# A graph network's second layer: the nodes' own edges as a dense stage, attributes closed up on the chip

## The chip, the cores and the metric

One core of a Trainium2 chip runs the whole program. Its engines are named PE (matrix products; PEld is its weight load), DVE (vector), ACT (activation), POOL (GpSimd) and SP (sync, which here issues most DMAs). The metric is the device time of one execution in microseconds (us); the time before is the median of three runs.

## The reference

A graph has 12,500 nodes of 64 values and 212,500 edges, sorted by target. 200,000 edges are random pairs in both directions; the other 12,500 are the nodes' own edges (source = target), one for each node. Each edge has 8 attributes and one of 16 types. What is computed, cut to what matters:

```python
h = relu(layernorm(x))
x = x + segment_sum(h[src] @ weight[etype], dst)            # first layer
h = relu(layernorm(x))
msg_in = concat([h[src], h[dst], edge_attr])                # second layer
x = x + segment_sum(relu(msg_in @ W1 + b1) @ W2 + b2, dst)
```

The second layer is done as a = h @ W1[:64] and b = h @ W1[64:128] + b1 for each node, then relu(a[src] + b[dst] + attr @ W1[128:]) for each edge. The sum over a node's edges is taken before the product with W2.

## The kernel before, in words

Edges are handled in tiles of 128, one edge to a partition, and tiles in groups of G = 4. For every tile POOL issues one indirect DMA (`gather`, line 737) that reads the 128 source rows of 64 values into a buffer; 14 such group buffers rotate (`land`, line 303).

**First layer** (`first_layer`, line 960). Own edges need no gather here: they are put into the table directly from the node's row (`begin`, `some`). The other edges are first closed up, that is, moved to the front where own edges were taken out. `compact` (line 487) does it on DVE: the number of places that a word must move is written in binary, and for each bit a mask is taken (`bitwise_and`) and the words are shifted under it (`copy_predicated`). POOL then stores the result to HBM as `edges_c` (source, type and target of each kept edge). `codes` reads it back, turns it on PE and gives `src_c`, the sources by tile. There are 1563 tiles of kept edges; 28 of the 1563 are covered by the first 32 raw tiles, which leaves 1535 gathers. PE multiplies each tile with a one-hot matrix made by ACT, and DVE adds the product into a window of `table`. Every 8 groups two blocks of 128 nodes are done, and `finish` (line 776) multiplies them with the weights of the types, adds x (held in `x_sb`), normalizes, and writes rows a and b to HBM (`a_rows`, `a_early`, `b_rows`).

**Second layer** (`second_layer`, line 1090). It uses all 212,500 edges in their original order: 1661 tiles, 416 groups, with sources `src_i`, targets within the window `local` and `dst_l`, and attributes `attr_t`, all prepared on the host and loaded. For a group, POOL gathers rows of a; PE forms b[dst] + attr @ W1c in one product from a window of 40 b rows plus 8 rows of weights (`b_win`) and a one-hot matrix with 8 rows of attributes under it (`of_edges`); DVE adds the two (`z`), ACT takes the relu (`hid`), PE sums over targets (`pa`), and DVE adds into a window of `sums`. Every 8.5 groups `results` (line 1069) multiplies two blocks with W2, adds x from `x_sb` and writes the output.

**The order.** Each engine's instructions stand in the order in which this code issues them: the class `InOrder` (line 316) hangs each one behind the last of its engine. All these instructions so have line 325 in the profile, and are told apart by their tiles. Preparation runs beside the first layer: generators such as `prepare` and `open_step` are advanced by one step for each tile (`for i in range(G)` at line 1041), and `yield from rest(n)` is a distance of n steps. Since POOL's stores stand in this order too, a store that waits holds back the gathers behind it.

`in_any_order` (line 1218) is a slow path for other kinds of input. It is in the program, but does not run here.

Of the kernel before, what the change touches and what calls it, by code (L numbers as in the profile page):

```python
# [40 lines left out]
F32 = mybir.dt.float32  # L41
# [37 lines left out]
AHEAD2 = AHEAD + 28  # L79
NGR = NT // G  # L80
NTR = -(-E // P)
# [20 lines left out]
LPARTS = EP // (P * LROW)  # L102
LOOPS_UPTO = [0, 2560, 5632, 8704, NB * P]
# [24 lines left out]
BS = 2  # L128
GS2 = 17
# [6 lines left out]
FIN = [-(-GS2 * (k + 1) // 2) + SLACK - 1 for k in range(NREG)] + [408, 412, NGR - 1]  # L136
STEP = [sum(f < g for f in FIN) for g in range(NGR)]
# [5 lines left out]
def bounds():  # L143

    least, most = [(0, 0)], [(0, 0)]
    for k in range(NFIN - 1):
        b0, nb = BLOCKS[k]
        end = (b0 + nb) * P

        x = (FIN1[k] + 1 - SHIFT) * G * P  # L150
        least.append((x + end, end))
        ahead = end + AHEAD - WT
        if x + ahead < E:
            most.append((x + ahead, ahead))
        x = (FIN[k] + 1) * G * P
        least.append((x, end))
        most.append((min(x, E) - 1, end + AHEAD2 - W))

    most.append((RAWE, RAWE - CUT * P))
    most.append((RAWE - 1, SN + AHEAD - WT))  # L160
    for c in range(1, PARTS):
        most.append((c * P * ROW, c * P * ROW - UPTO[c] * P))
    for q in range(1, LPARTS):
        least.append((q * P * LROW, LOOPS_UPTO[q]))
    return least, most
# [28 lines left out]
def gnn_kernel(  # L194
    ctx: ExitStack, tc, x, src, dst, etype, attr, src_t, dst_t, attr_t, rows_c, rows_l, raw_c, raw_f, first, last, step_t, step_c, least, most, w_rel, w1, b1, w2, b2, out
# [11 lines left out]
    dst_l = dram.tile([NGR, G * P], BF16, name="dst_l")  # L207
# [10 lines left out]
    x_sb = keep.tile([P, NB * D], F32, name="x_sb")  # L218
    x3 = x_sb.rearrange("p (b d) -> p b d", d=D)
    tail = N - (NB - 1) * P  # L220

    def load_x(b0, Q):

        full = min(b0 + LB, NB - 1)
        Q.dma_start(x3[:, b0:full, :], x[b0 * P : full * P].rearrange("(b p) d -> p b d", p=P))
        if b0 + LB == NB:
            V.memset(x3[:, NB - 1, :], 0.0)
            Q.dma_start(x3[:tail, NB - 1, :], x[(NB - 1) * P :])
# [3 lines left out]
    NCK = 3 * PARTS + 4 * LPARTS + 4  # L232
# [22 lines left out]
    def layer_norm(pool, b0, nb, name):  # L255
# [44 lines left out]
    def in_order():  # L300
        with ExitStack() as c2:
# [82 lines left out]
            local = own.tile([P, NT], F32, name="local")  # L384
            sums = [own.tile([DA, SN + AHEAD2], F32, name=f"sums{k}") for k in range(2)]
            first_row = own.tile([1, NGR], I32, name="first_row")
            src_i = own.tile([P, NT], I32, name="src_i")

            place_row = own.tile([1, NGR], I32, name="place_row")
            w1ab = own.tile([P, 2, D], F32, name="w1ab")  # L390
            b1_bc = own.tile([P, D], F32, name="b1_bc")
            w2b = own.tile([DA, D], F32, name="w2b")

# [14 lines left out]
            def weights():  # L408
# [5 lines left out]
                Q_.dma_start(t_loop[N:, :].rearrange("n o -> o n"), none)  # L414
                yield
                Q_.dma_start(first_row, first.unsqueeze(0))
                Q_.dma_start(place_row, step_t[::G].unsqueeze(0))
# [18 lines left out]
            def local_targets():  # L436

                n = NGR // RB
                d = prep.tile([n, RB, G * P], I32, name="local_d", bufs=1)
                f = prep.tile([n, RB], I32, name="local_f", bufs=1)  # L440
                o = prep.tile([n, RB, G * P], BF16, name="local_o", bufs=1)
                Q_.dma_start(d, dst[:EP].rearrange("(n g e) -> n g e", n=n, g=RB))
                Q_.dma_start(f, first.rearrange("(n g) -> n g", n=n))
                yield from rest(8)
                for g in range(RB):
                    V_.tensor_tensor(o[:, g, :], d[:, g, :], f[:, g : g + 1].to_broadcast([n, G * P]), op=ALU.subtract)
                    yield
                Q_.dma_start(dst_l.rearrange("(n g) e -> n g e", n=n), o)
                Q_.dma_start(src_i, src_t)
                for t in sums:  # L450
                    V_.memset(t, 0.0)
                V_.tensor_scalar(first_row, first_row, 0.0, float(N), op0=ALU.max, op1=ALU.min)
                V_.tensor_tensor(place_row, first_row, place_row, op=ALU.subtract)
                yield
                V_.tensor_scalar(place_row, place_row, 0.0, float(SN + AHEAD2 - W), op0=ALU.max, op1=ALU.min)
                yield

            def sources_of_last(of, pool):

                for g in of:  # L460
                    s_bc = pool.tile([P, G * P], I32, name="s_bc", bufs=1)
                    Q_.dma_start(s_bc, src[g * G * P : (g + 1) * G * P].unsqueeze(0).to_broadcast([P, G * P]))
# [7 lines left out]
            def locals_of(c):  # L470

                n = NT // NCH
                cs = slice(c * n, (c + 1) * n)
                d = prep.tile([P, n], I32, name="local_e", bufs=1)
                f = prep.tile([P, n // G], I32, name="local_w", bufs=1)
                Q_.dma_start(d, dst_t[:, cs])
                Q_.dma_start(f, first[c * n // G : (c + 1) * n // G].unsqueeze(0).to_broadcast([P, n // G]))
                yield from rest(8)
                V_.tensor_tensor(
                    local[:, cs].rearrange("p (g k) -> p g k", k=G),  # L480
                    d.rearrange("p (g k) -> p g k", k=G),
                    bc(f, 2, G, [P, n // G, G]),
                    op=ALU.subtract,
                )
                yield

# [289 lines left out]
            def finish(k, psA):  # L776
# [3 lines left out]
                long = nb == BS  # L780
                if long:
                    yield from rest(2)
# [21 lines left out]
                x_b = x3[:, b0 : b0 + nb, :]  # L804
                V_.tensor_tensor(x_b, x_b, pT[:, :nb, :], op=ALU.add)
                st = wk.tile([P, nb, 6], F32, name="s_st")
# [3 lines left out]
                for i in range(nb):  # L810
                    V_.bn_stats(st[:, i, :], x3[:, b0 + i, :])
# [81 lines left out]
            def verdict(psA):  # L893
                span = prep.tile([NGR // G, 2, G], I32, name="v_span", bufs=1)
                bad = prep.tile([NGR // G, G], F32, name="v_bad", bufs=1)
# [4 lines left out]
                Q_.dma_start(span[:, 0, :], first.rearrange("(n g) -> n g", g=G))  # L900
                Q_.dma_start(span[:, 1, :], last.rearrange("(n g) -> n g", g=G))
# [4 lines left out]
                V_.scalar_tensor_tensor(  # L906
                    bad, span[:, 1, :], -float(W), span[:, 0, :], op0=ALU.add, op1=ALU.is_ge,
                    accum_out=next(odds_of)[: NGR // G],
                )
# [34 lines left out]
            def beside_part(c, psA):  # L944
# [6 lines left out]
                if c == 1:  # L951
                    yield from local_targets()
                    yield from weights_of_attributes()
                if c == 5:
                    yield from sources_of_last(range(2), wk)
                yield from locals_of(c)
# [3 lines left out]
            def first_layer(psA, loops_0):  # L960
# [5 lines left out]
                open_step, coming, fresh = iter(()), iter(()), iter(())  # L966
                n_of, oh_of, rows_of, pa_of = {}, {}, {}, {}
# [37 lines left out]
                for it in range(NG1 - RAWG + L1_ADD[1]):  # L1005
                    g = it + RAWG
                    if g < NG1:
                        k = (g - SHIFT) * G
                        if it == 0 or k in UPTO:
                            c = sum(k >= b for b in UPTO[1:])  # L1010
                            for _ in coming:
                                next(fresh, None)
                            coming = beside_part(c, psA)
                        if it % 56 == 4 and it // 56 < NB // LB:
                            load_x(it // 56 * LB, Q_)
# [24 lines left out]
                    for j in range(max(len(now), len(adds))):  # L1040
                        for i in range(G):
# [9 lines left out]
                            next(coming, None)  # L1051
                        if j < len(adds) and adds[j] in FIN1:
# [3 lines left out]
                            for _ in fresh:  # L1056
                                next(coming, None)
                            if k + 1 < NFIN:
# [4 lines left out]
                for _ in coming:  # L1063
                    pass
# [3 lines left out]

            def results(k, ps):
                (b0, nb), t = BLOCKS[k], sums[k % 2]  # L1070
                po = ps.tile([P, BS, D], F32, name="po", bufs=1)
# [5 lines left out]
                V_.tensor_tensor(o[:, :nb, :], po[:, :nb, :], x3[:, b0 : b0 + nb, :], op=ALU.add)  # L1077
                if k + 2 < NFIN:
                    V_.memset(t[:, AHEAD2:], 0.0)
# [4 lines left out]
                else:  # L1084
                    S_.dma_start(
                        out[b0 * P : (b0 + nb) * P].rearrange("(b p) d -> p b d", p=P), o[:, :nb, :]
                    )
                yield

            def second_layer(ps):  # L1090
# [3 lines left out]
                open_step = iter(())  # L1094
                a_of, n_of, oh_of, pz_of, hid_of, pa_of = {}, {}, {}, {}, {}, {}
                at, at_b = {}, {}
                of_z, of_hid, of_pe, of_add = (turns(lag, NGR) for lag in (L2_Z, L2_HID, L2_PE, L2_ADD))
                for it in range(NGR + L2_ADD[1]):

                    g = it  # L1100
                    if g < NGR:
                        if g % RG == 0:
                            at_b.update(enumerate(windows(first_row, g, PAD_DST, Q_), g))
                        if g % RB == 0:
                            local_bc = wk2.tile([W, RB * G * P], BF16, name="local_bc", bufs=3)
                            Q_.dma_start(
                                local_bc,
                                dst_l[g : g + RB, :].rearrange("g e -> (g e)").unsqueeze(0).to_broadcast([W, RB * G * P]),
                            )
                            of_edges = wk2.tile([WE, RB * G * P], F32, name="of_edges", bufs=3)  # L1110
                            Q_.dma_start(of_edges[W:, :], attr_t[:, g * G * P : (g + RB) * G * P])
# [571 lines left out]
```

## Time and profile before

| | |
|---|---|
| median of three runs | 4086.79 us (4086.44 to 4087.43) |
| the profiled execution | 4087.75 us, its span 4085.9 us |
| POOL busy | 3083.5 us (75%), 3274 instructions |
| PE busy | 2422.0 us (59%) |
| ACT busy | 1640.5 us (40%) |
| DVE busy | 1146.0 us (28%) |
| granted TensorE clock | 0.523 |
| gathers of the first layer | from 50.9 to 2002.0 us |
| gathers of the second layer | from 2002.4 us; of a_rows from 2022.3 to 4075.7 us |

The page gives for each group of instructions the tiles written and read (out<-in), the shape, how many there are, their busy time, the mean duration of one, and the time that the engine sat idle before them with what ended it. "issue" means that nothing visible was waited for. An indirect DMA on POOL is the time in which POOL builds the transfer; the transfer itself follows. In the line of slices each digit is the busy share, in tenths, of a fortieth of the span.

### The profile page before, as it was taken

Reading aid. Unit: us, or ns where it says so; the run is one execution under the profiler, and the core shown is the slowest. Engines: PE = TensorE matmul, PEld = TensorE weight load, DVE = VectorE, ACT = ScalarE, POOL = GpSimd, SP = SyncE. Lnnn points to the kernel's source line nnn. Section 1 sums busy time; section 2 is a strip of 40 time slices with the busy share of each in tenths; the row PEclk is TensorE's granted clock in tenths of the full one; section 3 lists DMA queues with packets and bytes.
Section 4 is the critical chain, followed back from the end, with each engine's and each line's share of the span. In section 5 each row is a group of like instructions: output and inputs, shape, how many; then the busy total and the mean of one; then the engine's idle time right before and its main releaser. Section 6 shows DMA issues by size and latency. Waiting matters only on the chain. (4 is left out here: it accounts for less than half of the span.)

```text
span 4085.9 us, 49975 instructions
## 1 busy us (share of the span) xinstructions
PE 2422.0 (59%) x14840; PEld 1853.3 (45%) x14840; DVE 1146.0 (28%) x4671; ACT 1640.5 (40%) x3222; POOL 3083.5 (75%) x3274
## 2 busy tenths in 40 slices
PE   1655655555555555556686666666666666666655
PEld 0433333333333333333475555555555555555555
DVE  7533334333333333333211111111111111111111
ACT  6754545454545454545333222322232222322222
POOL 7777777777777777777777777777777777777776
PEclk9655555555555555555555555555555555555555
DMA  4222222121222222121222121111111112111111
GB/s 124 48 44 64 42 48 44 40 46 40 51 40 45 42 45 42 38 41 37 48 46 42 42 42 44 42 42 42 42 42 42 42 41 44 41 42 42 42 39 36
DMA packets 233554, 184.50 MB, mean 45 GB/s; under 512 B 162969, under 2 KB 171680, under 8 KB 232336
## 3 DMA queue, kind: packets, MB, share of 16 engines
q0 software_dynamic: 104320, 107.70, 14.1%
q1 hardware_dynamic: 115655, 70.30, 6.5%
q10 hardware_dynamic: 13298, 3.20, 0.4%
q8 instruction: 121, 1.98, 0.2%
q14 instruction: 160, 1.31, 0.1%
HBM read 162.74 MB, written 18.20 MB: 44 GB/s over the span
## 5 line engine op out<-in xcount | busy, mean ns | idle before, releaser
L325 POOL DMA_INDIRECT rows<-a_rows,src_i x1645 | 1552.2, 944 | 501.4 <-issue 428.9
L325 POOL DMA_INDIRECT rows<-h_rows,src_c x1535 | 1456.9, 949 | 468.2 <-issue 390.4
L325 PE MATMUL pa<-oh_r,rows 128*64 128x96 f32 x6140 | 836.2, 381 | 780.8 <-DMA rows<-h_rows,src_c 701.9
L325 PE MATMUL pz<-b_win,of_edges 48*128 48x64 f32 x3322 | 819.0, 424 | 686.3 <-ACT of_edges L325 682.1
L325 PEld LDWEIGHTS pz<-b_win,of_edges 48*128 48x128 f32 x3322 | 739.3, 324 | 735.7 <-ACT of_edges L325 712.0
L325 PEld LDWEIGHTS pa<-oh_r,rows 128*64 128x64 f32 x6140 | 472.4, 204 | 1193.8 <-DMA rows<-h_rows,src_c 848.8
L325 ACT ACTIVATE hid<-z 128x256 f32<-128x256 f32 x416 | 172.9, 416 | 1429.7 <-DVE z L325 1399.3
L325 DVE TENSOR_TENSOR z<-pz,rows 128x256 f32<-128x256 f32 x416 | 176.3, 424 | 1652.4 <-DMA rows<-a_rows,src_i 1520.3
L325 ACT ACTIVATE off_r<-iota_s,code 128x192 bf16<-128x192 f32 x1535 | 568.1, 441 | 0.0
L325 DVE TENSOR_TENSOR table<-table,pa 128x96 f32 x1567 | 395.6, 252 | 368.6 <-PE pa L325 262.1
L325 PE MATMUL pa<-oh,hid 128*65 128x40 f32 x3322 | 456.8, 312 | 38.3 <-ACT hid L325 27.2
L325 PEld LDWEIGHTS pa<-oh,hid 128*65 128x65 f32 x3322 | 395.9, 226 | 88.6 <-ACT hid L325 30.8
L325 ACT ACTIVATE oh_r<-off_r 128x768 f32<-128x768 bf16 x392 | 330.2, 842 | 211.5 <-PE pa L325 203.6
L325 DVE SCALAR_TENSOR_TENSOR table<-b_rel,rsel,hT 128x256 f32<-128x256 f32 (+1 forms) x400 | 171.6, 467 | 401.8 <-PE hT L325 391.6
L325 ACT ACTIVATE off<-local_bc,neg_w 40x1024 bf16<-40x1024 bf16 x208 | 235.8, 1134 | 21.5 <-DMA local_bc<-dst_l 12.9
L325 ACT ACTIVATE of_edges<-off 40x1024 f32<-40x1024 bf16 x208 | 219.7, 1056 | 6.5
L325 PE MATMUL pT<-table,wrel 128*64 128x256 f32 (+1 forms) x800 | 200.0, 596 | 2.1 <-DVE table L325 2.1
L325 DVE TENSOR_TENSOR oh<-local,iota_p 128x160 f32<-128x160 f32 x416 | 128.5, 310 | 0.0
L325 DVE TENSOR_TENSOR x_sb<-x_sb,pT 128x128 f32<-128x128 f32 (+1 forms) x50 | 14.2, 284 | 394.5 <-PE pT L325 394.5
L325 ACT COPY table<-table 128x1024 f32<-128x1024 f32 x49 | 51.2, 1045 | 143.0 <-DVE table L325 143.0
L325 ACT ACTIVATE s_rs<-s_mv,eps 128x2 f32<-128x2 f32 (+1 forms) x50 | 14.8, 296 | 230.9 <-DVE s_mv L325 230.9
L325 DVE TENSOR_TENSOR sums<-sums,pa 65x40 f32 x416 | 75.2, 181 | 46.1 <-PE pa L325 33.8
(193 smaller groups left out, 1049.6 us busy)
## 6 DMA issues: line engine op xcount, KB each, us to landing
rows<-a_rows,src_i POOLq DMA_INDIRECT x1645
rows<-h_rows,src_c POOLq DMA_INDIRECT x1535
local_bc<-dst_l SPq DMA_DIRECT2D x104, 160.0 KB
of_edges<-in_attr_t SPq DMA_DIRECT2D x104, 64.0 KB
b_win<-b_rows SPq DMA_DIRECT2D x416, 10.0 KB
b_rel<-t_loop SPq DMA_DIRECT2D x48, 128.0 KB
l_in<-in_rows_l SPq DMA_DIRECT2D x4, 1009.5 KB
b_h<-h_rows SPq DMA_DIRECT2D x48, 64.0 KB
```

The costliest lines, as they stand in the source:

```text
L325: last_ins[self.engine] = getattr(self.engine, name)(*args, **kw)
```

## The change

The second layer now uses the closed-up edges of the first: `src_c`, 391 groups (1563 tiles, the last group of three), 8 groups to two blocks. Everything that came from the host for it (`src_t`, `dst_t`, `attr_t`, `first`, `last`) is gone. In its place:

- `places_of` makes `first_row`, `local` and `dst_l` of each part from `edges_c`. It replaces `local_targets` and `locals_of`.
- `kept` closes up the attributes of the kept edges on DVE, four times, 128 rows of 432 edges with 8 words each, and POOL stores them (`attr_c`).
- `loop_attrs` picks out the attributes of the own edges, four times, and POOL stores them (`attr_l`).
- `turn` reads 16 tiles of attributes back (pieces of 8 words), turns them on PE, copies them on ACT and writes `turned_c` or `turned_l`: 99 and 7 times.
- These run beside the first layer: `attrs` takes a step for every second tile, `turns_of_attrs` for every tile.
- `own_edges`, once for two blocks, computes the own edges' relu(a + b + attr @ W1c) densely, turns it and writes it into `sums` before the windows of those blocks are added. The window ahead grows from 156 to 256 columns.
- x is no longer held: `finish` loads two blocks (`x_b`) and writes the sum to HBM (`x_mid`); `results` reads it back (`x_r`).

The core of the diff:

```diff
-AHEAD2 = AHEAD + 28
+BS = 2
+AHEAD2 = BS * P
+KWIN = 432
+KCL = 400
+SUB = 16
+IN_SUB = 3
+            def kept(q):
...
+                a = prep.tile([P, KWIN * EA], F32, name="k_a", bufs=1)
+                load_halves(a, attr, q, EA, KWIN)
...
+                a3 = a.rearrange("p (e c) -> p e c", c=EA).bitcast(I32)
+                for k in range(5):
+                    n = 1 << k
+                    V_.tensor_single_scalar(move, v, n, op=ALU.bitwise_and)
+                    half = KWIN // 2
+                    for e0, e1 in ((0, half), (half, KWIN - n)):
+                        V_.copy_predicated(
+                            a3[:, e0:e1], wide(move[:, e0 + n : e1 + n], [P, e1 - e0, EA]), a3[:, e0 + n : e1 + n]
+                        )
+                        yield
+                    if k < 4:
+                        V_.copy_predicated(v[:, : KWIN - n], move[:, n:], v[:, n:])
+                    yield
+                yield from store(attr_c, to, a[:, : KCL * EA], rest)
+                closed.append(q)
+            def loop_attrs(q):
...
+                for h in range(2):
...
+                    load_halves(a[:, : m * SUB * EA], attr, q, EA, m * SUB, h * m * SUB)
+                    yield from rest(14)
+                    a4 = a[:, : m * SUB * EA].rearrange("p (b e c) -> p b e c", e=SUB, c=EA).bitcast(I32)
...
+                    for k in range(4):
+                        n = 1 << k
+                        V_.tensor_single_scalar(m3, v3, n, op=ALU.bitwise_and)
+                        V_.copy_predicated(
+                            a4[:, :, : SUB - n], wide(m3[:, :, n:], [P, m, SUB - n, EA]), a4[:, :, n:]
+                        )
+                        yield
...
+                for k in range(7):
+                    n = 1 << k
+                    V_.tensor_single_scalar(v2[:, 1], v2[:, 0], n, op=ALU.bitwise_and)
+                    V_.copy_predicated(top_i[:, : last - n], wide(v2[:, 1, n:], [P, last - n, EA]), top_i[:, n:])
+                    if k < 6:
+                        V_.copy_predicated(v2[:, 0, : last - n], v2[:, 1, n:], v2[:, 0, n:])
+                    yield
+                yield from store(attr_l, to, top[:, :LN].rearrange("p s c -> p (s c)"), rest)
+            def turn(of, t0, n, into, psA):
+                t = prep.tile([P, 16, EA], F32, name="u_in", bufs=3)[:, :n]
+                words = of[t0 * P * EA : (t0 + n) * P * EA, :]
+                Q_.dma_start(t, words.rearrange("(t p c) o -> p t (c o)", p=P, c=EA))
+                yield
+                yield from take(bank)
+                by_c = psA.tile([P, P], F32, name="hT", bufs=1)[: n * EA]
+                T_.transpose(by_c, t.rearrange("p t c -> p (t c)"), ident)
+                yield
+                o = prep.tile([P, P], F32, name="u_out", bufs=2)[: n * EA]
+                S_.copy(o, by_c)
+                bank.clear()
+                Q_.dma_start(into[t0 * EA : (t0 + n) * EA, :], o)
+                yield
+            def own_edges(b, t, col, ps):
...
+                for i in range(BS):
+                    T_.matmul(po[:, i, :], lhsT=at[:, i, :], rhs=w1c, start=True, stop=True)
+                yield
+                V_.tensor_tensor(ab[:, 0], ab[:, 0], po, op=ALU.add)
+                V_.tensor_tensor(ab[:, 0], ab[:, 0], ab[:, 1], op=ALU.add)
+                S_.activation(h[:, :, :D], ab[:, 0], AF.Relu)
+                yield
+                pl = both[:DA, : BS * P]
+                for i in range(BS):
+                    T_.matmul(pl[:, i * P : (i + 1) * P], lhsT=h[:, i, :], rhs=ident, start=True, stop=True)
+                yield
+                V_.tensor_copy(t[:, col : col + BS * P], pl)
...
-                        a_of[g], n_of[g] = gather((a_early if g < EARLY else a_rows)[:, :], src_i, g, NTR)
+                        a_of[g], n_of[g] = gather((a_early if g < EARLY else a_rows)[:, :], src_c, g, NTC)
```

In `first_layer`, the two new streams are advanced here (the lines around it are as before):

```diff
                             next(coming, None)
+                            if i % 2:
+                                next(aside, None)
+                            next(turning, None)
```

## The prediction

> **What bounds the kernel now.** I read the busy table first, then the slices, then the groups of POOL by shape, its waits, and last the timeline of POOL and DVE together.
>
> ```profile
> POOL 7777777777777777777777777777777777777776
> L325 POOL DMA_INDIRECT rows<-a_rows,src_i x1645 | 1552.2, 944 | 501.4 <-issue 428.9
> L325 POOL DMA_INDIRECT rows<-h_rows,src_c x1535 | 1456.9, 949 | 468.2 <-issue 390.4
> L325 POOL DMA_INDIRECT edges_c<-c_out,c_to x16 | 14.6, 913 | 4.9 <-issue 4.0 <-DVE table L325 0.6 <-DVE r_mv L250 0.3
> ```
>
> POOL shows the same 7 in every slice. Its 3252 indirect DMAs stand in an unbroken row: (1552.2 + 501.4) / 1645 = 1.248 us from one start to the next in the second layer, 0.944 of it busy and 0.30 issue, and in its list of waits the longest single wait is 0.7 us. PE waits for the gathers in both layers (701.9 us for h_rows; DVE's z 1520.3 us for a_rows). So the time is the number of POOL's indirect DMAs times their pace, and an edit counts if it changes that number or that pace. The chain that ended last begins only behind the last gather, and says no more.
>
> The pace differs a little: 944 ns in the second layer, 949 in the first. The timeline shows why.
>
> ```profile
> 622.06 0.85 DVE L325 SCALAR_TENSOR_TENSOR l_f<-l_f 128x672 f32<-128x672 f32 x1
> 622.26 1.46 POOL L325 DMA_INDIRECT rows<-h_rows,src_c  x1 [0.30 <-issue]
> ...
> 102.19 0.41 DVE L325 COPY_PREDICATED c_v<-c_move,c_v 128x223 int32<-128x223 int32 x1
> 102.25 1.15 POOL L325 DMA_INDIRECT rows<-h_rows,src_c  x1 [0.30 <-issue]
> ...
> 52.85 0.86 DVE L325 MAX8 l_top<-l_f 128x8 f32<-128x672 f32 x1
> 53.40 0.94 POOL L325 DMA_INDIRECT rows<-h_rows,src_c  x1 [0.30 <-issue]
> ```
>
> The columns are start, duration, instruction. A gather that starts while a DVE instruction with two SBUF inputs is under way ends 0.81 to 0.82 us after that instruction's end: 622.06 + 0.85 = 622.91, and 622.26 + 1.46 = 623.72; 102.60 and 103.40. Behind MAX8, one SBUF input and as long, nothing happens (0.94). So a gather is lengthened by (what is left of the DVE instruction at its start) - 0.13 us, and the next gather follows 0.30 us later, so that nothing is caught up. With a gather every c = 1.249 us, at a random place against it, a DVE instruction of length L costs POOL on average (L-0.13)^2/2c if L-0.13 is under c, and L-0.13-c/2 if it is over. Test on this trace: summed over all such instructions of the first layer after 90 us this gives 7.5 us; the gathers there exceed 944 ns by 7.2 us in all. For the formula that is a good match, though with lengths up to 0.86 us only.
>
> **What the change removes from POOL.** The second layer gathers 1547 tiles in place of 1645 (391 groups, the last of three tiles): 98 x 1.248 = **-122.3 us**.
>
> **What it adds to POOL.** Sixteen stores (eight attr_l, eight attr_c), at the edges_c row (14.6 + 4.9) / 16 = 1.22 us: **+19.5**. The t_loop stores, 128 bytes a row, take 914 ns, edges_c, 1.6 KB a row, 913: size does not show. attr_c writes 12.8 KB a row; if that doubled its eight, +7 more.
>
> **What it adds in POOL's way.** Closing up attributes is DVE work with two SBUF inputs, in the first layer. Lengths from these rows:
>
> ```profile
> L325 DVE COPY_PREDICATED c_v<-c_move,c_v 128x223 int32<-128x223 int32 x7 | 2.9, 410 | 0.2
> L325 DVE COPY_PREDICATED c_v<-c_move,c_v 128x208 int32<-128x208 int32 x7 | 2.8, 394 | 0.2
> L325 DVE TENSOR_TENSOR c_f<-c_f 128x224 f32<-128x224 f32 x14 | 5.5, 389 | 0.2
> L325 DVE TENSOR_TENSOR l_f<-l_f 128x672 f32<-128x672 f32 x4 | 3.4, 854 | 0.0
> ```
>
> From 224 to 672 elements 465 ns, so 1.04 ns an element; a predicated copy is 0.178 us + 1.04 n. The program holds, over four parts each of `kept` and `loop_attrs`:
> - 40 predicated copies of 1600 to 1728 elements (a half row of 8 words an edge): 1.85 to 1.98 us, 78 us busy; cost 1.17 to 1.22 each: 47.9.
> - 8 each of 2520, 2352, 2016 and 1344 elements: 2.80, 2.63, 2.28, 1.58 us; cost 2.05, 1.87, 1.52, 0.82: 50.2.
> - 28 of 496 to 1000 elements, 1.08 us on average: 0.37 each: 10.4.
> - 16 tensor_tensor of 672, 0.855 us: 0.21 each: 3.4.
> - the short ones (40 copies of the counts, 8 of 432, 8 of 126, `places_of`): 4.2.
>
> Together 235 us of DVE and **+116 us** of POOL; the removed `local_o` and `local` rows take off 0.7 by the same formula. DVE has room: 723 of 1910 us busy between 90 and 2000 us. The two ends, if the formula's mean fails: the 72 copies over 1.5 us cost at least L-0.13-1.249 each and at most L-0.13, so 0.62 us less or more each, 45 us in all. The 80 one-input mask instructions (bitwise_and, 0.2 to 0.4 us by c_move's 302 ns) hold some gathers too: by the formula +1.3.
>
> The Trainium skill ("SBUF — State Buffer", Who interferes with whom) says that VectorE and GpSimd share a pair of SBUF ports, exclusively and for a whole instruction; but it infers that tensor_tensor does not hold up descriptor generation, only copies and tensor_scalar in a two-port mode do. This trace contradicts that: 1.43 to 1.55 us beside two-input instructions. By the page's inference the added holds would be the 1.3 alone and the time about 3986.
>
> **What lies beside.** Everything else is on engines that wait for POOL, and I cost it at nothing:
> - PE: 106 + 16 transposes in the first layer at 0.40 to 0.48 us (hT, pab rows), some 55 us against 780.8 us of waiting for h_rows; in the second layer 49 times four small products, near 90 us, against 686.3 us of waiting, and 392 products fewer each of pz and pa.
> - ACT: 122 copies of about 0.3 us in the first layer; in the second 49 activations more, 12 pairs off and of_edges fewer.
> - SP and DMA: about 210 issues of 0.4 us for the turning, 50 + 50 + 50 for x_b, x_mid, x_r, 147 for the own rows. A turning read has 2048 pieces of 32 bytes; x_sb's load, 1792 pieces of 256 bytes, is through 5 us after issue, and one such read falls on about 6.5 us. A core's DMA engines are at 0.22.
> - The cover for all this is 14 groups of row buffers, 70 us of POOL: z lags the gathers by 1.7 us in the second layer, and by at most 28 us at its start, where SP now has about eight DMAs more. Without the cover a late load would cost POOL its full lateness.
> - The end: the last group has 3 tiles in place of 1; its pa and z rows (0.31 each product) add under 1 us.
>
> New waits on POOL's queue: the first store of each pair follows its last DVE step at once, and for attr_c also the turning reads in flight; behind it queue the gathers. The table adds that stand at the same place in the order end 8 to 23 us before POOL gets there, and the last step takes 2 us. So 0 now; at worst the 8 to 10 us of that lead each, eight times.
>
> **Sum**, on the profiled execution (span 4085.9, 4087.75 in all): 4087.75 - 122.3 + 19.5 + 116 - 0.7 + 1.3 = 4101.6; where a burst of copies fills DVE, its next copy starts 0.6 to 1.0 us behind the last, before POOL's next start at 1.11, which costs some 0.3 more for about 15 of them: +4.5, so 4106. The runs' median is 1.0 lower: **4105**. POOL's gain is given back beside DVE.
>
> **Rivals.**
> 1. Forecast, the holds cost what the formula says: 4085 to 4130. Chance 0.57.
> 2. Faster: the long copies hold POOL less than the short ones suggest. One mechanism, where a copy starts against a gather: DVE's steps follow PE, which follows the gathers, so a fixed distance could put the start just behind a gather's start. The lower end, -45: 4060. With no hold at all it is 3986. It decides as soon as the holds sum to less than 95 us. For it: no row is over 0.86 us. Against: the 1560 table adds, which pace these steps, end at any place against the gathers (137 to 181 in each tenth), and the 35 c_v copies lie nearly as evenly. Chance 0.21.
> 3. Waits in place of the gain: `kept` brings 25 us of DVE within about eight groups (40 us, 15 busy already), the lead is used up and POOL waits at the first stores, on DVE and on the reads; SP in turn waits for the stores' landing, and the loads behind it come late. Eight times 5 us: 4145; at 10 us, 4185. For it: SP already waits 78.8 us for t_loop stores, longest 28.9. Against: POOL, slowed by the holds, gives DVE more time. Chance 0.22.
> 4. That it does not do what it says: the program's POOL row shows 1547 gathers; no chance given.
>
> **Numbers.** About 0.2% (8 us) is what a measurement can tell from no change. Of case 1 a quarter lies within 8 us of before (4079 to 4095), of case 2 a tenth: same 0.16. Faster 0.19, slower 0.65. The range takes case 2's phase end and case 3's middle: 4060 to 4150; outside lie no hold at all (0.06) and heavy waits (0.08). Both signs hold much, so case 1 alone: 4085 to 4130.
>
> **What would show it.** In the profile after: 1547 a_rows gathers at 944 ns, and h_rows gathers at a mean near 949 + 116/1535 = 1.02 us, issue still 0.30; k_a copies of 1.9 to 2.8 us in the timeline with a gather of 2 us or more beside them; L1 longer by about 140 us, L2 shorter by 122; POOL's waits without a DVE line over a few us. Wrong it would be if k_a copies run beside gathers of 0.94, if POOL waits at attr_c, or if the pace of the second layer leaves 1.25.

## The result, and the profile after

The changed kernel takes 4123.51 us (median of four runs, 4122.70 to 4125.71), the kernel before 4086.80: ratio 1.0091, 95% interval 1.0073 to 1.0108. It is slower by 36.7 us where 18 were forecast; the time lies inside the range of 4060 to 4150 and inside case 1's own range. The profiled execution took 4123.03 us, its span 4121.2.

First the page after: POOL's share by slices, then its groups (busy, mean ns of one, idle before), and from the groups by shape the two new stores.

```profile
POOL 7777777777777777777777777777777777777776
L320 POOL DMA_INDIRECT rows<-h_rows,src_c x1535 | 1582.7, 1031 | 474.2 <-issue 393.8
L320 POOL DMA_INDIRECT rows<-a_rows,src_c x1547 | 1462.5, 945 | 471.5 <-issue 402.3
```

```profile
L320 POOL DMA_INDIRECT attr_c<-k_a,k_to x8 | 7.3, 913 | 2.4 <-issue 1.8 <-DVE table L320 0.6
```

POOL still bounds in every slice. The second layer lost its 98 gathers: its a_rows gathers take 1933.7 us from first to last, 119.7 less. The first layer does the same 1535 gathers, but one takes 1031 ns in place of 949: from first to last they take 2105.5 us in place of 1951.1, 154.4 more. These two make the difference but for 0.6 us. An attr_c store with 12.8 KB a row takes 913 ns like every other, and waits 0.30 us.

The timeline of POOL and DVE shows where 82 ns a gather come from.

```profile
397.43 0.94 POOL L320 DMA_INDIRECT rows<-h_rows,src_c  x1 [0.30 <-issue]
397.91 3.02 DVE L320 COPY_PREDICATED k_a<-k_i,k_a 128x2520 int32<-128x2520 int32 x1
398.68 3.05 POOL L320 DMA_INDIRECT rows<-h_rows,src_c  x1 [0.30 <-issue]
402.03 0.94 POOL L320 DMA_INDIRECT rows<-h_rows,src_c  x1 [0.30 <-issue]
402.50 2.79 DVE L320 COPY_PREDICATED k_a<-k_i,k_a 128x2352 int32<-128x2352 int32 x1
403.28 2.79 POOL L320 DMA_INDIRECT rows<-h_rows,src_c  x1 [0.30 <-issue]
```

Both readings agree with the rule that was read from rows under 0.9 us: 397.91 + 3.02 = 400.93, and the gather ends 0.80 us behind that, at 401.73. The gather that is under way when a copy starts (397.43) is not touched. Over the whole trace 72 indirect DMAs start under one of the 72 k_a copies, and exceed their usual time (944 ns a gather, 913 a store) by 1456 ns on average, 104.8 us in all; under the 28 k_top copies 25, 16.6 us in all.

### The profile page after: what moved, and what is told of

It reads as the page before. It is cut to its first block, busy times and chain, and to the rows that moved or that the text cites. A ratio compares the mean times of both kernels' runs of the same rounds, so it can differ in the third digit from the quotient of the medians.

```text
span 4121.2 us, 51359 instructions
## 1 busy us (share of the span) xinstructions
PE 2465.1 (60%) x14962; PEld 1880.9 (46%) x14962; DVE 1409.8 (34%) x5048; ACT 1644.0 (40%) x3344; POOL 3137.5 (76%) x3192
## 2 busy tenths in 40 slices
DMA packets 530030, 232.82 MB, mean 56 GB/s; under 512 B 432073, under 2 KB 467653, under 8 KB 527691
## 5 line engine op out<-in xcount | busy, mean ns | idle before, releaser
L320 POOL DMA_INDIRECT rows<-h_rows,src_c x1535 | 1582.7, 1031 | 474.2 <-issue 393.8
L320 POOL DMA_INDIRECT rows<-a_rows,src_c x1547 | 1462.5, 945 | 471.5 <-issue 402.3
L320 PE MATMUL pa<-oh_r,rows 128*64 128x96 f32 x6140 | 804.1, 376 | 840.9 <-DMA rows<-h_rows,src_c 763.2
L320 PE MATMUL pz<-b_win,of_edges 48*128 48x64 f32 x3126 | 771.2, 424 | 352.6 <-ACT of_edges L320 348.0
L320 PEld LDWEIGHTS pz<-b_win,of_edges 48*128 48x128 f32 x3126 | 695.7, 324 | 413.4 <-ACT of_edges L320 389.7
L320 PE MATMUL pa<-oh,hid 128*65 128x40 f32 x3126 | 428.9, 312 | 36.9 <-ACT hid L320 22.3
L320 PEld LDWEIGHTS pa<-oh,hid 128*65 128x65 f32 x3126 | 372.5, 226 | 83.6 <-ACT hid L320 29.4
L320 DVE COPY_PREDICATED k_a<-k_i,k_a 128x1728 int32<-128x1728 int32 (+2 forms) x72 | 161.2, 2240 | 1.8
L320 ACT COPY u_out<-hT 128x128 f32<-128x128 f32 (+2 forms) x106 | 27.9, 263 | 238.8 <-PE hT L320 206.1
L320 ACT ACTIVATE hid_l<-o_ab 128x128 f32<-128x128 f32 x49 | 15.3, 311 | 255.7 <-DVE o_ab L320 255.7
```

The source lines that it names most:

```text
L320: last_ins[self.engine] = getattr(self.engine, name)(*args, **kw)
```

## The experiments

**Theory 1** is the forecast's: a gather that starts while DVE reads two operands from SBUF waits until that instruction is through. **Theory 2**: the first layer is longer because of the added DMA traffic. **Theory 3**: DVE being busy holds the gathers, whatever its operands are. The first four kernels shared one chip, on which the kernel before took 4087.49 us; the last three another one, 4086.93.

**e1_mask: the masks in PSUM.**

```diff
-                v, move = i_[:, 0, :KWIN], i_[:, 1, :KWIN]
+                v = i_[:, 0, :KWIN]
+                move = psA.tile([P, KWIN], I32, name="pm", bufs=1)
...
-                hT_p = psA.tile([P, P], F32, name="pab", bufs=2)
+                hT_p = psA.tile([P, P], F32, name="pab", bufs=1)
...
-                    pab = psA.tile([P, 2, D], F32, name="pab", bufs=2)
+                    pab = psA.tile([P, 2, D], F32, name="pab", bufs=1) if i else turned[:, : 2 * D].rearrange("p (s d) -> p s d", d=D)
```

(`loop_attrs` likewise; the lines that hand `psA` down are left out.)

> The masks of the wide predicated copies (k_a, k_top, and of the short copies of the move counts beside them) lie in a PSUM tile in place of k_i and k_v, so that each copy reads one operand from SBUF; to free a bank for it, the first pab of a finish step shares the bank of pT. Theory 1 (a gather that starts while VectorE runs an instruction with two SBUF inputs is lengthened by what is left of it less 0.13 us): by the lengths measured in the changed kernel the k_a copies cost 106.9 us, k_top 11.5, k_i 2.6; they go, 4123.5 - 121 = about 4002 us, and the gathers of h_rows come down from 1031 ns to about 952 ns mean. Theory 2 (the first layer is longer because of the added DMA traffic, the 32-byte reads of u_in and the attribute loads): nothing of that is touched, 4120 to 4125 us. Theory 3 (the hold goes by VectorE being busy, whatever its operands are): also about 4123 us, with the gathers still lengthened beside the k_a copies.

Measured: 3995.67 us (3994.12 to 3996.10), ratio 0.9776 (0.9759 to 0.9792). Its groups by shape and its timeline:

```profile
L320 DVE COPY_PREDICATED k_a<-pm,k_a 128x2520 int32<-128x2520 int32 x8 | 24.4, 3053 | 0.3
L320 POOL DMA_INDIRECT rows<-h_rows,src_c x1535 | 1460.4, 951 | 472.7 <-issue 370.3 <-DMA rows<-h_rows,src_c 88.8 <-PE pa L320 3.7
```

```profile
379.43 3.05 DVE L320 COPY_PREDICATED k_a<-pm,k_a 128x2520 int32<-128x2520 int32 x1
380.22 0.95 POOL L320 DMA_INDIRECT rows<-h_rows,src_c  x1 [0.30 <-issue]
381.47 0.94 POOL L320 DMA_INDIRECT rows<-h_rows,src_c  x1 [0.30 <-issue]
382.72 0.94 POOL L320 DMA_INDIRECT rows<-h_rows,src_c  x1 [0.30 <-issue]
```

The copy is as long as before (3053 ns against 3024), and two gathers start and end beneath it at their usual 0.94. In all 122 gathers and stores start under a k_a copy, with a mean excess of 0 ns. DVE is as busy (1420.0 us against 1409.8) and the DMA packets are the same 530,030: theories 2 and 3 fall for the bulk of the loss. The time is 6 us under the expectation, 7.4 on the profiled executions; the traces put 1.6 of it into the second layer (below), 1.5 into shorter idle time of POOL, and the rest into more removed holds than the formula counted.

**e2_no_wide: no wide copies.**

```diff
-                        V_.copy_predicated(
-                            a3[:, e0:e1], wide(move[:, e0 + n : e1 + n], [P, e1 - e0, EA]), a3[:, e0 + n : e1 + n]
-                        )
...
-                        V_.copy_predicated(
-                            a4[:, :, : SUB - n], wide(m3[:, :, n:], [P, m, SUB - n, EA]), a4[:, :, n:]
-                        )
...
-                    V_.copy_predicated(top_i[:, : last - n], wide(v2[:, 1, n:], [P, last - n, EA]), top_i[:, n:])
```

> The wide predicated copies (k_a and k_top) are left out, so the attributes are stored as loaded and the rows are not closed up; loads, masks, short copies, stores, turning and own edges stay. Theory 1: the holds of 106.9 + 11.5 us go, 4123.5 - 118 = about 4005 us. Theory 2 (added DMA traffic): 4115 to 4123 us. Theory 3 (VectorE busy): about 4005 us too.

Measured: 4000.15 us (3999.43 to 4001.45), ratio 0.9787 (0.9770 to 0.9803). Leaving the copies out is worth no more than moving their masks (4.5 us less, 1.8 of it the holds of the short k_i copies, whose masks stay in SBUF here). The wide copies take 193 us of DVE (161.2 + 31.5), and nothing shows that they cost POOL anything but through the operand.

**e4_split: the same copies in pieces.**

```diff
-                    for e0, e1 in ((0, half), (half, KWIN - n)):
-                        V_.copy_predicated(
-                            a3[:, e0:e1], wide(move[:, e0 + n : e1 + n], [P, e1 - e0, EA]), a3[:, e0 + n : e1 + n]
-                        )
+                    for h0, h1 in ((0, half), (half, KWIN - n)):
+                        for e0 in range(h0, h1, 54):
+                            e1 = min(e0 + 54, h1)
+                            V_.copy_predicated(
+                                a3[:, e0:e1], wide(move[:, e0 + n : e1 + n], [P, e1 - e0, EA]), a3[:, e0 + n : e1 + n]
+                            )
                         yield
...
+                        for b in range(0, m, 3):
                             V_.copy_predicated(
-                            a4[:, :, : SUB - n], wide(m3[:, :, n:], [P, m, SUB - n, EA]), a4[:, :, n:]
+                                a4[:, b : b + 3, : SUB - n], wide(m3[:, b : b + 3, n:], [P, 3, SUB - n, EA]), a4[:, b : b + 3, n:]
```

> Each k_a copy is cut into pieces that are issued one behind the other without a step between: the 40 of kept into four of 432 elements (0.62 us by 0.13 + 1.14 ns an element), the 32 of loop_attrs into seven of 192 to 360 elements (0.35 to 0.54 us); the same elements are copied. Theory 1, where only the piece under way when the gather starts holds it: (L - 0.13)^2 / (2 x 1.249) each, 160 x 0.096 + 56 x 0.188 = 15.4 + 10.5 = 25.9 us in place of 106.9, so 4123.5 - 81 = about 4042 us. If a gather waits until the whole train of pieces is through (the hold goes by the time VectorE is continuously busy): 4123 us or some 20 us more, as the pieces add about 330 fixed parts of some 0.1 us. Theory 2 (added DMA traffic): 4120 to 4125 us.

Measured: 4035.84 us (4035.28 to 4038.54), ratio 0.9875 (0.9859 to 0.9892). The timeline, with seven pieces on one line:

```profile
457.68 0.94 POOL L320 DMA_INDIRECT rows<-h_rows,src_c  x1 [0.30 <-DMA rows<-h_rows,src_c]
458.14 2.70 DVE L320 COPY_PREDICATED k_a<-k_i,k_a 128x288 int32<-128x288 int32 x7
458.93 1.23 POOL L320 DMA_INDIRECT rows<-h_rows,src_c  x1 [0.30 <-issue]
460.46 1.17 POOL L320 DMA_INDIRECT rows<-h_rows,src_c  x1 [0.30 <-issue]
461.93 0.94 POOL L320 DMA_INDIRECT rows<-h_rows,src_c  x1 [0.30 <-issue]
```

A gather waits for the piece under way and not for the train, though DVE goes on without a break. The pieces hold the gathers by 19.9 us in all (25.9 expected, 104.8 uncut), while DVE is busy 189.8 us with them in place of 161.2. The hold goes by the length of one instruction.

**e7_runs and e3_pieces: the idle stretches.** POOL's list of waits shows the rest of the first layer's loss: the longest wait for a row transfer was 0.3 us before and is 2.2 after. Four stretches, behind the gathers that start at 1182.7, 1341.5, 1532.1 and 1703.4 us, are over 1 us, 6.67 us in all. The windows around the second of them:

```profile
1310.00:1322.00 12.00, 6.02 (x41) 3.36 (x40) 4.25 (x20) 7.24 (x17) 8.95 (x11) 0.50 0.38 76
1322.00:1334.00 12.00, 6.21 (x52) 4.42 (x52) 6.01 (x21) 4.99 (x12) 9.01 (x10) 0.50 0.53 108
1334.00:1346.00 12.00, 3.69 (x26) 1.98 (x26) 2.04 (x8) 3.48 (x8) 8.04 (x9) 0.50 1.10 179
```

The columns are the window, its length, the busy time of PE, PEld, DVE, ACT and POOL, the granted clock, the DMA engines' share and GB/s. The share adds up the whole time of each packet that starts in the window, so it can pass 1. In the last window the DMA engines are full, and PE, DVE and ACT run dry, as the rows come late. Two things were issued at 1332 to 1334 us: `kept`'s attribute load (1.73 MB) and two u_in reads of 2048 pieces each. First the reads:

```diff
-                Q_.dma_start(t, words.rearrange("(t p c) o -> p t (c o)", p=P, c=EA))
+                Q_.dma_start(t, words.rearrange("(p t c) o -> p t (c o)", p=P, c=EA))
```

> Each u_in tile is read as one run of n x 32 bytes per partition (512 bytes for n = 16) in place of n runs of 32 bytes 4 KB apart: same bytes, 16 times fewer packets; the turned tables then hold the edges in another order, so the second layer's attributes are not those of its edges. Theory 1: the only part of the 37 us that these reads carry is the four idle stretches of GpSimd of 1.2 to 2.2 us beside pairs of u_in reads (5.5 us over their normal 0.30 each): about 4118 us. Theory 2 (the added DMA traffic is the cause of most of the longer first layer): the packets fall from 530 thousand by some 200 thousand and the time by 50 us or more, below 4075 us.

Measured: 4120.36 us (4117.92 to 4122.51), ratio 1.0080 (1.0063 to 1.0097). The packets fall from 530 to 331 thousand, and theory 2 falls a second time. But the stretches stay, three of 1.3 to 1.6 us and one of 0.7, 4.9 us in all against 6.7: the small pieces are at most a part of them. Then the load:

```diff
-                load_halves(a, attr, q, EA, KWIN)
+                for c0 in range(0, KWIN, KWIN // 4):
+                    load_halves(a[:, c0 * EA : (c0 + KWIN // 4) * EA], attr, q, EA, KWIN // 4, c0)
+                    yield from rest(2)
```

> The attribute load of kept (two transfers, 1.73 MB at once) is issued in four pieces of 432 KB with two steps (about 5 us) after each; nothing else. Theory 1 with its refinement (the four idle stretches of GpSimd of 1.17, 1.77, 1.54 and 2.19 us behind gathers come from these loads filling the DMA engines, as they lie beside them with 32-byte and with 512-byte reads of u_in alike): the stretches shrink to the usual 0.30 us, 6.67 - 1.20 = 5.5 us less, about 4118 us. Rival (the 32-byte reads of u_in alone fill the engines): the stretches stay, 4123 us. The mean of the h_rows gathers stays at about 1031 ns either way.

Measured: 4115.50 us (4113.38 to 4116.77), ratio 1.0070 (1.0056 to 1.0083), 8.0 us under the changed kernel. Its groups of POOL:

```profile
L320 POOL DMA_INDIRECT rows<-h_rows,src_c x1535 | 1581.7, 1030 | 468.4 <-issue 379.8 <-DMA rows<-h_rows,src_c 79.5 <-PE pa L320 2.4
```

The idle time is 468.4 us, that of the kernel before (468.2), and no stretch is left; the mean gather stays at 1030 ns. So the stretches need the load at once, 5.8 us. That it is enough is not shown: `loop_attrs` issues eight loads of 1.34 MB between 92 and 994 us, before the first u_in read, and behind them POOL's longest wait is 0.65 us. On the profiled executions, which lie 9.7 us apart, the rest is about 2 us of holds that fell out shorter and 1.7 us in the second layer, where 23 gathers in place of 36 exceed 960 ns; the next experiment shows what lengthens them.

**e5_sums: the second layer's own loss.** Its mean went from 944 to 945 ns, on the trace 943.6 to 945.4, 1547 times: 2.7 us. The timeline of the changed kernel names the neighbour:

```profile
2319.38 0.29 DVE L320 COPY sums<-sums 65x256 f32<-65x256 f32 x1
2319.49 0.99 POOL L320 DMA_INDIRECT rows<-a_rows,src_c  x1 [0.30 <-DMA rows<-a_rows,src_c]
2320.79 0.95 POOL L320 DMA_INDIRECT rows<-a_rows,src_c  x1 [0.30 <-issue]
```

```diff
-                                V_.tensor_copy(sums[(k + 1) % 2][:, :AHEAD2], sums[k % 2][:, n : n + AHEAD2])
+                                S_.copy(sums[(k + 1) % 2][:, :AHEAD2], sums[k % 2][:, n : n + AHEAD2])
```

> The copy of the overlap between the two sums tiles in the second layer (65x256, one SBUF input, 300 ns, on VectorE) goes to ScalarE. Theory 1 widened to this copy (32 of the 36 lengthened a_rows gathers lie beside it, 77 ns each, 2.5 us in all): the mean of the a_rows gathers falls from 945.4 to 943.7 ns and the second layer by 2.5 us, about 4121 us. Rival (the gathers there are lengthened by the own edges' loads or by their two additions): the 2.5 us stay, 4123 us. What ScalarE takes for it is beside the gathers.

Measured: 4119.26 us (4117.47 to 4122.35), ratio 1.0080 (1.0066 to 1.0093). The time alone can't tell it from the changed kernel, but the trace does: the a_rows gathers have their mean of 943.5 ns back, two of them exceed 960 ns in place of 36, and they take 2.8 us less from first to last. 42 gathers had started under the 49 copies, lengthened by 58 ns on average, 2.4 us in all. Where the copy stays on DVE it does not always cost that much: in e1_mask 42 gathers start under it too, later in the copy, and it costs 0.6 us.

**e6_all: the three edits together** (e1_mask, e3_pieces, e5_sums).

> The three edits together: masks in PSUM, the attribute load of kept in pieces, the sums copy on ScalarE. Theory 1: 3995.7 with the masks alone, less the idle stretches that this run still had (5.8 us in five, 1.5 of it usual: 4.3) and less its lengthened second layer (0.7 us): about 3991 us, 2.35% below the kernel before. Rival (the stretches stay, or the loads in pieces delay the closing up so that the turning ends behind the first layer): 3996 us or more.

Measured: 3990.49 us (3990.32 to 3990.91), ratio 0.9764 (0.9751 to 0.9777), 96.4 us faster than the kernel before and 133 faster than the changed one. Its page:

```profile
L320 POOL DMA_INDIRECT rows<-h_rows,src_c x1535 | 1462.0, 952 | 468.4 <-issue 374.3
L320 POOL DMA_INDIRECT rows<-a_rows,src_c x1547 | 1459.7, 944 | 471.5 <-issue 385.3
```

Both layers are back at nearly the means of before, 952 ns for 949 and 944 for 944, with 98 gathers fewer and 16 stores more: 98 x 1.248 - 16 x 1.22 = 102.8 us, less some 5 for the remaining holds of the new code; by the profiled executions it is 97.4.

## Why the prediction was right in direction and half of the size

By the forecast's own steps, on the profiled executions (35.3 us measured, 18.3 forecast, a miss of 17.0, of which 8 are holds, 6 idle time beside transfers and 2.6 the `sums` copy):

- **Removed gathers**: -119.7 against -122.3. The 98 x 1.248 stands. The 2.6 are the `sums` copy, which the forecast had not looked at. The change widened it from 156 to 256 columns (241 to 300 ns), but what differs most is its place: before, 6 gathers start under the 49 copies, and one is lengthened, by 62 ns; after, 42 do. That the width brought this about is not shown. "Everything else" was costed at nothing because it runs on engines that wait for POOL. That reason holds for what follows POOL, and not for what stands in its way.
- **Stores**: 16 x 1.21 = 19.4, as forecast (19.5). The doubled price for long rows didn't come, nor the waits at the stores: rival 3's mechanism fell.
- **Holds, the step that was mis-sized**: 129 us in the first layer (136.8 less 7.8 before, counted against 944 ns a gather and 913 a store) against 121 (116 - 0.7 + 1.3 + 4.5). The parts:
  - The long copies took 161 us of DVE in place of 152, as the line 0.178 us + 1.04 ns an element, read from rows of at most 672 elements, was too flat: 1728 elements took 2.09 us, not 1.98, and 2520 took 3.02, not 2.80. So the k_a copies cost 104.8 us, not 98.1 (47.9 + 50.2). With the measured lengths the formula gives 106.9 us for them. A gather that starts well beneath one is lengthened by what is left of it less 0.16 us, not 0.13; with that the formula comes to 104.9.
  - The k_top copies cost 16.6 us, not 10.4, at nearly the forecast length (31.5 us busy, 30.2 forecast); 16.4 to 17.1 in three further kernels that kept them and the k_a copies. They don't fall at random places against the gathers, which the formula assumes: of the 25 gathers beneath them 17 start 0.21 to 0.24 us after the copy does. In e1_mask, where nothing is held, none of 23 does; so the hold has a part in setting their place, and by what chain wasn't tried.
  - All other holds together came to 7.6 us, where the forecast had 12.7 (3.4 + 4.2 + 1.3 + 4.5 - 0.7).
- **Transfers at nothing, the step that failed**: 6.0 us of idle time (474.2 against 468.2), nearly all in the four stretches. The forecast looked at the reads of 32 bytes; without the load of 1.73 MB at once there are no stretches (e3_pieces), and the cover of 14 row buffers, 70 us by the forecast, did not keep POOL going, though PE's longest wait for the late rows was 7.5 us. Whether the load alone would do it, without the u_in reads beside it, is not shown. What POOL itself waits for in the stretches is open: the trace names the transfer of the rows as what came last, and nothing was tried on it.
- The remaining 0.6 us lie at the ends. The median is 0.5 us above the profiled run; 1.0 below was assumed.

Two figures of the forecast's working are off and change nothing: by its own formula the 40 copies cost 1.09 to 1.22 us each, not 1.17 to 1.22 (their sum of 47.9 stands), and in the trace before, the gathers after 90 us exceed 944 ns by 7.8 us, not 7.2, still near the formula's 7.5.

Rival 2 (holds smaller by phase) fell: the holds came to 129 us, not under 95. But that the formula's mean fits k_a so well is in part luck. The places are not even: behind the start of 31 of the 72 copies the next gather starts 0.62 to 0.94 us later, where even places would give 18. Their mean, 0.63 us, happens to be half of the pace, and that is all that the formula uses of it for copies longer than the pace. The forecast's main claim is shown by e1_mask: with the operand in another place the same 1535 gathers take 1460.4 us in place of 1582.7. The forecast listed what is in POOL's way, and did not ask how cheaply it could be moved out of it.

The Trainium skill ("SBUF — State Buffer", Who interferes with whom) says that a VectorE instruction with at most one SBUF input, outside the two-port modes, does not contend with GpSimd, and that a plain copy may take the shared ports. Here the masks in PSUM (a mean excess of 0 ns) and the `sums` copy (58 ns over 42 gathers, none on ScalarE) agree with both. The forecast set the trace against the section's inference on `tensor_tensor` and descriptor generation, and rightly; it left out that the same section has an instruction with two SBUF inputs contend with a GpSimd instruction that reads SBUF. A gather's row numbers (`src_c`) lie in SBUF, and the holds agree with that sentence.

## What to carry to other kernels

Where POOL's indirect DMAs set the pace, list for every added DVE instruction how many operands it reads from SBUF and how long it is, not only whether DVE has room: a hold costs what is left of the instruction, less some 0.15 us here, when a gather starts beneath it. Then move one operand to PSUM, give plain copies to ACT, or at least cut the instruction into short ones. And where a large load runs beside small transfers that something waits for, try it in pieces: here that was worth 5.8 us for four loads of 1.73 MB.

## What the runs showed of the hardware

- The hold comes from the operands and not from the operation: the same COPY_PREDICATED of 3.05 us lengthens a gather by over 2 us with its mask in SBUF and not at all with its mask in PSUM.
- It goes by single instructions: in a train of seven pieces that takes 2.70 us without a break, a gather waits for the rest of one piece (1.23 and 1.17 us in place of 0.94).
- The other way no hold shows: the eight copies of 2520 elements all start while a gather has 0.13 to 0.94 us still to run, and take 3.01 to 3.05 us, no longer than with their mask in PSUM (3.03 to 3.06).
- A copy of 65x256 with one SBUF input holds gathers too (58 ns on average in the changed kernel, 15 in e1_mask), so counting inputs is not quite enough.
- A predicated copy with a broadcast mask takes as long with the mask in PSUM (2102 ns at 1728 elements) as in SBUF (2093).
- An indirect store takes 913 ns for 64 rows of 12.8 KB as well as of 1.6 KB.
